# Second attention: the mirrored blocks of a chunk made by TensorE transposes, copied an item later

## The chip, the cores and the metric

The kernel runs on one core of one Trainium2 chip. The metric is the device time of one execution in microseconds, the median of several runs. Before the change it is 1772.9 us, the median of 3 runs (1772.55 to 1773.56).

## The reference

The input is 8 images of 128 channels and 48 x 48 positions (N = 2304 tokens). Layer 0 is a causal attention with projections; layer 1 is a second attention of the normalized tokens with themselves, and a recurrent layer behind it. The change concerns the second attention alone. Cut to what matters:

```python
def _L1_attn_ref(x):                       # x: (batch, tokens, 128), layer-normed
    attn = jnp.einsum('bnd,bmd->bnm', x / TEMPERATURE, x)
    attn = jax.nn.softmax(attn, axis=-1)
    out = jnp.einsum('bnm,bmd->bnd', attn, x)
    return out
...
x = x + _L0_conv_ref(_gn(x), ...)          # causal attention
t = _to_tokens(x)
t = t + _L1_attn_ref(_ln_t(t))             # second attention
t = t + _L1_ffn_ref(_ln_t(t), ...)         # batch norm and a recurrence over the tokens
```

The logits of the second attention are x times x transposed, so the matrix of logits is symmetric, and so are its exponentials before they are divided by the row sums.

## The kernel before, in words

All work is in fp32. The 2304 tokens of an image are 18 blocks of 128 (`NB`), or 6 chunks (`NQ`) of 384 columns (`QC`), each of 3 blocks (`QB`). Two classes make the two attentions: `Causal` (line 984) and `Full` (line 1118, the one that is changed). Each gives a list of items, one for each pair of a chunk j of queries and a block m of keys. In `Full`, an item is one of two kinds:

- *direct*: `begin` multiplies the block m by the chunk j (L1214, tile `s`, a PSUM bank of the pool `ps_s`), and ScalarE takes the exponential into a tile `p` of the pool `pp` (6 buffers), with a constant bias and with the sum over the columns into `rows[:, m, j]` (L1216). Then `product` multiplies `p` by the tokens of block m and adds it to the chunk's result `o` (L1228).
- *turned*: where the same pair of chunks was made before with the roles exchanged. VectorE has transposed the earlier `p` in pieces of 32 (L1177) and summed it (L1185), a DMA has stored it (`e`, L1157), another has loaded it (`g`, L1148); `begin` then makes no logits and `product` multiplies `g` (L1224).

Direct items of chunk j are those of the later chunks and of chunk j itself. The three of chunk j itself, the *own* items, are computed in full, 384 columns each, though of their nine blocks of 128 x 128 three are transposes of three others. I call the own items O0, O1, O2, other direct items D, and turned ones T. Chunk 0 begins O0 O1 O2 D D and so on. In later chunks the own items come last among the direct ones, and T are spread between by position:

```
1 D D D T D D D D D T D D D D O0 T O1 O2
2 D T D D T D D T D D T D D T O0 O1 T O2
3 D T D T D T D T D T D T O0 T O1 T O2 T
4 T D T T D T T D T T O0 T T O1 T T O2 T
5 T T O0 T T T T T O1 T T T T T O2 T T T
```

(The first figure is the chunk; O2 of chunk 5 stands among items of the next image's causal attention, which are put in between, at lines 1417 to 1421.)

The order of all work is written by hand (`manual_schedule`). One loop (lines 1426 to 1437) goes over the items of all images: at step n it calls `begin` of item n, then `product` of item n − 3 (`LAG = 3`), then `st.tick()`, which can issue up to two steps of the side chains. Each engine carries out its instructions in the order of issue:

```python
            if n < len(stream):
                part, j, what, first, last = stream[n]
                ready[n] = part.begin(j, what, first)
            if n >= LAG:
                part, j, what, first, last = stream[n - LAG]
                ...
                part.product(j, what, o[part, j], *ready.pop(n - LAG), first, last)
                ...
            st.tick()
```

`Stream` (line 548) is a planner: `spend` advances a planned TensorE clock, `then` plans when the other engines will be done, and a side chain's next step is issued once its planned time has come. Side chains carry the residuals, norms, projections (`pj`, L874 and L877) and the DMAs between them. A chunk's chain after its last product turns `o` back by TensorE transposes (`of_t`, L934), divides by the sums (`dn` from `rows`, L1254, and `ts`, L1259), and later multiplies by the first weight of the recurrent layer (`wx`, L1320); ScalarE has copies in it, `of` (L1246), `t2c` (L1341) and `wx` (L1326). The causal chains have `dn` (L1072) and `tb` (L934, read by L1105). Their PSUM tiles come from the pool `ps_t` (`psum_t`), which has two buffers used in turn.

Of the kernel before, what the change touches and what calls it, by code (L numbers as in the profile page):

```python
# [14 lines left out]
F32 = mybir.dt.float32  # L15
AF = mybir.ActivationFunctionType
ALU = mybir.AluOpType
AX = mybir.AxisListType
# [32 lines left out]
def general_path(ctx: ExitStack, tc: tile.TileContext, x, wq, bq, wk, bk, wv, bv, w_ffn, v_ffn, gamma, beta, pe, out):  # L51
# [44 lines left out]
    with ExitStack() as actx:  # L96
# [82 lines left out]
        def pop(n=1):  # L179
            for _ in range(n):  # L180
                if pend:
                    pend.popleft()()
# [195 lines left out]
        def full_attention(b, xhT, xh, done):  # L378
            xt = xbuf[b]
            LAG = 2  # L380

# [50 lines left out]
            for j in range(NQ):  # L432
                o = psum_o(f"o1_{b}_{j}")
                acc = work.tile([P, QC], F32, tag="acc", name=f"acc_{b}_{j}")
                ps = {}
                for m in range(NB + LAG):
                    if m < NB:
# [11 lines left out]
                    if j == 0 or m % 3 == 1:  # L449
                        pop()  # L450
                    if m >= LAG:
                        u = m - LAG
                        nc.tensor.matmul(o[:, :QC], xhT[:, u, :], ps.pop(u), start=(u == 0), stop=(u == NB - 1))
# [151 lines left out]
def fast_path(ctx: ExitStack, tc: tile.TileContext, x, pe, w_ffn, out, x_tok, w_qkv, w_pos, v_t, gamma_beta, flag):  # L605
    nc = tc.nc
    B, C, H, W = x.shape
    N = H * W
    P = 128
    assert C == P and N % P == 0  # L610
    NB = N // P
    CH = 512
    QC = 384
    NQ = N // QC
    QB = QC // P
    SCALE = 1.0 / math.sqrt(P)
    US = 4 / 2400.0
# [25 lines left out]
    ident = cpool.tile([P, P], F32, tag="ident", name="ident")  # L643
# [20 lines left out]
    with ExitStack() as actx:  # L664
# [11 lines left out]
        small2 = actx.enter_context(tc.tile_pool(name="small2", bufs=2))  # L676
# [4 lines left out]
        def psum_s(name):  # L681
            return ps_s.tile([P, CH], F32, tag="s", name=name)

        def psum_t(name):
            return ps_t.tile([P, CH], F32, tag="t", name=name)
# [13 lines left out]
        def psum_o(name):  # L699
            return ps_o.tile([P, CH], F32, tag="o", name=name)  # L700
# [28 lines left out]
        shift = apool.tile([P, 1], F32, tag="shift", name="shift")  # L729
# [46 lines left out]
        st = Stream()  # L776
# [207 lines left out]
        class Causal:  # L984
# [18 lines left out]
            def begin(self, j, m, first):  # L1003
                b = self.b
                if first:
                    st.finish(projected[b, j])
                    if j + EARLY < NQ:
                        project(b, j + EARLY)
                    if j == NQ - 1:
                        bounds(b)  # L1010
                off = self.offset(j, m)
                s = psum_s(f"s_{b}_{j}_{m}")
                nc.tensor.matmul(s[:, off:QC], keys[b][:, ts(m, P)], queries[b, j][:, off:], start=True, stop=True)  # L1013
                p = pp.tile([P, QC], F32, tag="p", name=f"p_{b}_{j}_{m}")
                nc.scalar.activation(p[:, off:], s[:, off:QC], AF.Exp, scale=SCALE)  # L1015
                ops = [("ACT", 0.16 + (QC - off) * 0.00085)]
                if m >= QB * j:
                    nc.gpsimd.tensor_mul(p[:, off : off + P], p[:, off : off + P], triu)  # L1018
                    ops.append(("POOL", 0.5))
                return p, st.then(st.spend((QC - off) * US), ops)  # L1020
# [97 lines left out]
        class Full:  # L1118
# [72 lines left out]
            def begin(self, j, what, first):  # L1191
                b = self.b
                if first and j == 0:
                    self.rows = small2.tile([P, NB, NQ], F32, tag="rows", name=f"rows_{b}")
                if j == 0:
                    st.finish(normed_chunks[b, what[1] // QB])
                if first and b + 1 < B:
                    if j == 1:
                        norm_chain[b + 1] = st.add(group_norm(b + 1))
                    if j == NQ - 2:  # L1200
                        st.finish(norm_chain[b + 1])
                        project(b + 1, 0)
                self.prefetch()
                if what[0] == "turned":
                    i, g = what[1:]
                    while (i, j) not in self.loaded:
                        while self.pairs[len(self.loaded)] not in self.stored:
                            self.store()
                        self.load()
                    return self.loaded[i, j][:, :, g, :, :].rearrange("p a m r -> p m a r"), 0.0  # L1210
                m = what[1]
                xh = x_hat[b][1]
                s = psum_s(f"s1_{b}_{j}_{m}")
                nc.tensor.matmul(s[:, :QC], xh[:, ts(m, P)], xh[:, ts(j, QC)], start=True, stop=True)  # L1214
                p = pp.tile([P, QC], F32, tag="p", name=f"p1_{b}_{j}_{m}")
                nc.scalar.activation(p, s[:, :QC], AF.Exp, bias=shift, accum_out=self.rows[:, m, j : j + 1])  # L1216
                return p, st.then(st.spend(QC * US), [("ACT", 0.58)])

            def product(self, j, what, o, p, ready, first, last):
                xhT = x_hat[self.b][0]  # L1220
# [13 lines left out]
            def after(self, j, o):  # L1234
                b, rows, tsum = self.b, self.rows, self.tsum
# [4 lines left out]
                if far:  # L1240
                    ot = turn_result(o, f"f_{b}_{j}", c, True)
                    at = st.then(st.now, [("DVE", 0.57)])
                    through = token_major(c, ot, f"f_{b}_{j}", "tof", 4)
                else:
                    o_sb = chunk_tile("o", f"of_{b}_{j}", c, 2)
                    nc.scalar.copy(o_sb, o[:, :QC])  # L1246
                    at = st.then(st.now, [("ACT", 0.5)])
# [3 lines left out]
                def sums():  # L1251

                    dn = small2.tile([P, QB], F32, tag="dn", name=f"dn_{b}_{j}")
                    nc.vector.tensor_reduce(dn, rows[:, QB * j : QB * (j + 1), : j + 1], AX.X, ALU.add)  # L1254
                    n = NQ - 1 - j
                    if n:
                        tp = psum_t(f"ts_{b}_{j}")
                        k = n * R * QB
                        nc.tensor.matmul(  # L1259
                            tp[:, :k], same.rearrange("p a c -> p (a c)"), tsum[j][:, :n, :].rearrange("p n k -> p (n k)"),  # L1260
                            start=True, stop=True,
                        )
                        own = small2.tile([P, NQ - 1, R, QB], F32, tag="own", name=f"own_{b}_{j}")
                        nc.vector.tensor_mul(
                            own[:, :n].rearrange("p n a g -> p (n a g)"), tp[:, :k], mine[:, :n].rearrange("p n a g -> p (n a g)")
                        )
                        more = small2.tile([P, QB], F32, tag="more", name=f"more_{b}_{j}")
                        nc.vector.tensor_reduce(more, own[:, :n].rearrange("p n a g -> p g (n a)"), AX.X, ALU.add)
                        nc.vector.tensor_add(dn, dn, more)
                    ri = small.tile([P, QB], F32, tag="ri", name=f"ri_{b}_{j}")  # L1270
                    nc.vector.reciprocal(ri, dn)
                    c["ri"] = ri
# [104 lines left out]
                else:  # L1377
# [7 lines left out]
                c["chain"] = self.before["chain"] = st.add([  # L1385
                    *through,
                    (sums, 0.15, [("DVE", 0.8)]),
                    (residual, 0.0 if far else 0.35, [("DVE", 3.2)]),
                    (rooted, 0.0, [("POOL", 0.9)]),
# [21 lines left out]


        LAG = 3
        stream = []
        for b in range(B):
            part, items = Causal(b), Causal.items()
# [5 lines left out]
            stream += [(part, *i) for i in items]  # L1422
            part = Full(b)
            stream += [(part, *i) for i in part.items()]
        ready, o = {}, {}
        for n in range(len(stream) + LAG):
            if n < len(stream):
                part, j, what, first, last = stream[n]
                ready[n] = part.begin(j, what, first)
            if n >= LAG:  # L1430
                part, j, what, first, last = stream[n - LAG]
                if first:
                    o[part, j] = psum_o(f"o_{n}")
                part.product(j, what, o[part, j], *ready.pop(n - LAG), first, last)
                if last:
                    part.after(j, o.pop((part, j)))
            st.tick()
# [10 lines left out]
    with ExitStack() as rctx:  # L1448
# [89 lines left out]
        for t in range(-WARM, LS):  # L1538
            s = t % TZ
# [28 lines left out]
        off = rc.tile([P, 1], F32, tag="off", name="off")  # L1568
# [11 lines left out]
@with_exitstack  # L1580
def conv_attn_hybrid_kernel(ctx: ExitStack, tc: tile.TileContext, args, laid):


    nc = tc.nc
    fpool = ctx.enter_context(tc.tile_pool(name="flag", bufs=1))
    flag = fpool.tile([1, 1], mybir.dt.int32, tag="flag", name="flag")
    x, w_ffn, pe, out = (args[i] for i in (0, 7, 11, 12))
    fast_path(tc, x, pe, w_ffn, out, *laid, flag)
    redo = nc.values_load(flag[0:1, 0:1], min_val=0, max_val=1, skip_runtime_bounds_check_because="the flag is the result of a comparison")
    with tc.If(redo > 0):  # L1590
        general_path(tc, *args)
# [41 lines left out]
```

## Time and profile before

| what | us |
|---|---|
| median of the runs | 1772.9 |
| the profiled execution, its own time | 1774.48 |
| its span, first to last instruction | 1772.5 |
| TensorE (PE) busy | 1742.7 |
| VectorE (DVE) busy | 1302.8 |
| ScalarE (ACT) busy | 764.8 |
| logits of direct items (L1214), 1008 matmul instructions | 410.4 |
| their products (L1228), 1008 | 404.1 |
| products of turned items (L1224), 720 | 281.3 |
| exponentials of direct items (L1216), 504 | 292.4 |
| reads of their accumulator, 504 | 97.2 |

An fp32 product is two matmul instructions, so the 504 direct items show as 1008. A matmul's recorded duration contains the time in which the next one already streams, so the spacing of starts says more on what it costs TensorE than its duration. PE is matmul, PEld the weight loads ahead of them. "Idle before" in a group's line is the time that the engine stood still just before its instructions, with what ended it. A transpose on TensorE is one matmul instruction whose weights are the block and whose moving operand is the identity.

### The profile page before, as it was taken

The page shows a single profiled execution, that of the slowest core. Times are in us where ns is not written, and L with a number is a line of the kernel's source. Part 1 is how long each engine was busy: PE and PEld are TensorE (multiplying, and loading weights), DVE is VectorE, ACT ScalarE, POOL GpSimd, SP SyncE. Part 2 cuts the span into 40 slices and gives each one's busy share as a digit, 9 for nine tenths or more (in the row PEclk, how much of TensorE's full clock was granted, in tenths as well). Part 3 has the DMA queues.
Part 4 walks back from the last instruction along what each step waited for, and adds up shares of the span by engine and source line. Part 5 has one row for each costly group of instructions (what it writes and reads, how often), then busy time and mean ns, then how long its engine had stood idle before and what let it go on. Part 6 is the DMA issues. An engine that isn't in the chain of part 4 may idle for free.

```text
span 1772.5 us, 22223 instructions
## 1 busy us (share of the span) xinstructions
PE 1742.7 (98%) x6231; PEld 1093.2 (62%) x6231; DVE 1302.8 (74%) x3363; ACT 764.8 (43%) x1842; POOL 195.2 (11%) x303
## 2 busy tenths in 40 slices
PE   8999999999999999999999999999999999999996
PEld 5666566665666566665666656665666656665565
DVE  4868668876887668786687767876687866877467
ACT  2344434443345434444344433454344543444455
POOL 1110011100110001100111001100011001110006
PEclk8999999999999999999999999999999999999998
DMA  4405672257533584156732575335941468116768
GB/s 140 138 23 187 182 204 94 87 184 188 145 103 128 159 226 141 34 176 182 200 99 80 188 192 152 106 111 161 237 129 50 160 183 214 45 65 198 194 211 216
DMA packets 206056, 262.00 MB, mean 148 GB/s; under 512 B 90113, under 2 KB 175010, under 8 KB 205412
## 3 DMA queue, kind: packets, MB, share of 16 engines
q1 hardware_dynamic: 204972, 257.47, 49.4%
q0 software_dynamic: 720, 2.62, 1.0%
q8 instruction: 52, 0.85, 0.2%
q14 instruction: 80, 0.66, 0.1%
q10 hardware_dynamic: 232, 0.40, 0.1%
HBM read 150.24 MB, written 110.17 MB: 147 GB/s over the span
## 4 chain that ended last, share of the span: by engine, by line
PE 96%; DMA 1%; DVE 1%; ACT 0%; issue 0%; SPq 0%; POOL 0%; ACTq 0%; POOLq 0%; DVEq 0%
PE o L1228 18%; PE s L1214 18%; PE s L1013 17%; PE o L1024 17%; PE o L1224 13%; PE pj L874 4%; PE pj L877 2%; PE z L1547 2%; PE wx L1320 2%; PE of_t L934 1%; PE tb L934 1%; PE pb L832 0%; DMA x<-in_x_dram 0%; PE dn L1072 0%; PE ts L1259 0%
## 5 line engine op out<-in xcount | busy, mean ns | idle before, releaser
L1216 ACT ACTIVATE p<-s,shift 128x384 f32<-128x384 f32 x504 | 292.4, 580 | 479.7 <-PE s L1214 464.2
L1015 ACT ACTIVATE p<-s 128x384 f32<-128x384 f32 (+2 forms) x504 | 231.8, 460 | 424.8 <-PE s L1013 377.5
L1214 PE MATMUL s<-xh 128*128 128x384 f32 x1008 | 410.4, 489 | 0.0
L1228 PE MATMUL o<-p,xhT 128*128 128x384 f32 x1008 | 404.1, 488 | 5.9 <-ACT p L1216 5.9
L1013 PE MATMUL s<-q,k 128*128 128x384 f32 (+2 forms) x1008 | 381.5, 460 | 0.2 <-DVE k L884 0.2
L1024 PE MATMUL o<-p,vT 128*128 128x384 f32 (+2 forms) x1008 | 377.4, 456 | 0.0
L1224 PE MATMUL o<-g,xhT 128*128 128x384 f32 x720 | 281.3, 488 | 1.1 <-DMA g<-e 1.1
L1228 PEld LDWEIGHTS o<-p,xhT 128*128 128x128 f32 x1008 | 188.9, 190 | 133.8 <-ACT p L1216 10.5
L1024 PEld LDWEIGHTS o<-p,vT 128*128 128x128 f32 x1008 | 188.8, 190 | 114.7 <-issue 0.6
L1214 PEld LDWEIGHTS s<-xh 128*128 128x128 f32 x1008 | 186.2, 190 | 115.3
L1013 PEld LDWEIGHTS s<-q,k 128*128 128x128 f32 x1008 | 182.6, 191 | 97.3 <-issue 1.0
L1039 DVE TENSOR_TENSOR acc<-acc,p 128x384 f32<-128x384 f32 (+2 forms) x408 | 208.8, 512 | 33.4 <-POOL p L1018 8.7
L1177 DVE STREAM_TRANSPOSE t<-p 128x384 f32<-128x384 f32 x360 | 187.3, 550 | 37.6 <-ACT p L1216 32.8
L1224 PEld LDWEIGHTS o<-g,xhT 128*128 128x128 f32 x720 | 133.2, 190 | 83.7 <-DMA g<-e 1.3
L1185 DVE TENSOR_REDUCE tsum<-t 128x12 f32<-128x1152 f32 x120 | 162.3, 1353 | 4.2
L879 DVE TENSOR_TENSOR z<-pj,pb 128x384 f32<-128x384 f32 x144 | 78.8, 547 | 108.8 <-PE pj L874 92.4
L1018 POOL TENSOR_TENSOR p<-p,triu 128x128 f32<-128x128 f32 x144 | 72.5, 505 | 606.2 <-ACT p L1015 475.2
L1294 POOL TENSOR_TENSOR roots<-ve_f,mhalf 128x3 f32<-128x3 f32 x48 | 40.7, 849 | 521.8 <-DVE ve_f L918 521.8
L1216 ACT ACTIVATION_READ_ACCUMULATOR p<-s,shift 128x1 f32 x504 | 97.2, 193 | 0.0
L874 PE MATMUL pj<-xn,wT 128*128 128x384 f32 x192 | 79.7, 500 | 1.4 <-DVE xn L867 1.4
L924 POOL TENSOR_TENSOR rs_c<-ve_c,mhalf 128x3 f32<-128x3 f32 x48 | 45.1, 939 | 216.2 <-DVE ve_c L918 213.6
L1321 DVE TENSOR_TENSOR scale<-wx,scale 128x384 f32<-128x384 f32 x46 | 25.4, 551 | 56.1 <-PE wx L1320 50.3
(264 smaller groups left out, 1485.6 us busy)
## 6 DMA issues: line engine op xcount, KB each, us to landing
e<-t SPq DMA_DIRECT2D x120, 576.0 KB
g<-e SPq DMA_DIRECT2D x480, 144.0 KB
pb<-posb_d SPq DMA_DIRECT2D x46, 576.0 KB
t1t<-in_x_tok_dram SPq DMA_DIRECT2D x48, 192.0 KB
t_d<-tt SPq DMA_DIRECT2D x184, 48.0 KB
t2x<-t_d SPq DMA_DIRECT2D x46, 192.0 KB
scale<-rs SPq DMA_DIRECT2D x46, 192.0 KB
x<-in_x_dram SPq DMA_DIRECT2D x14, 576.0 KB
```

The source lines that it names most:

```text
L874: nc.tensor.matmul(ps[:, :QC], wT[:, j, :], xn, start=True, stop=True)
L879: nc.vector.tensor_add(z, ps[:, :QC], c["pb"][:, j, :])
L1013: nc.tensor.matmul(s[:, off:QC], keys[b][:, ts(m, P)], queries[b, j][:, off:], start=True, stop=True)
L1015: nc.scalar.activation(p[:, off:], s[:, off:QC], AF.Exp, scale=SCALE)
L1024: nc.tensor.matmul(o[:, off:QC], vals[b][:, ts(m, P)], p[:, off:], start=first, stop=last)
L1039: nc.vector.tensor_add(a[:, off:], a[:, off:], p[:, off:])
L1177: nc.vector.transpose(t[:, :, :, g, :].rearrange("p b j r -> p j b r"), p.rearrange("p (j b r) -> p j b r", j=QB, b=R))
L1185: nc.vector.tensor_reduce(self.tsum[j][:, n - j - 1, :], t.rearrange("p b j m r -> p (b j) (m r)"), AX.X, ALU.add)
L1214: nc.tensor.matmul(s[:, :QC], xh[:, ts(m, P)], xh[:, ts(j, QC)], start=True, stop=True)
L1216: nc.scalar.activation(p, s[:, :QC], AF.Exp, bias=shift, accum_out=self.rows[:, m, j : j + 1])
L1224: nc.tensor.matmul(out_ap, xhT[:, QB * i + g, :], p, start=first, stop=last)
L1228: nc.tensor.matmul(o[:, :QC], xhT[:, what[1], :], p, start=first, stop=last)
```

## The change

In an own item n of the chunk (n = 0, 1, 2), only the columns from block n on are multiplied and exponentiated: 384 for O0, 256 for O1, 128 for O2. The missing blocks are made from the earlier own items: a function `mirror` takes a PSUM tile of `psum_t`, transposes into it one block (O1) or two (O2) on TensorE, and ScalarE copies them into the left part of `p`, with their sum over the columns into a new column 0 of `rows`. The other columns of `rows` move up by one; column 0 is set to zero by GpSimd once for each image, and the reduction of `rows` takes one column more. The loop keeps the mirrors in a list and issues that of item n at step n + 2, after `begin` of item n + 2 and ahead of `product` of item n − 1; the product of item n follows a step later, as before. 144 transposes and 96 copies are added, and the planner is given costs for them.

```diff
             def begin(self, j, what, first):
                 b = self.b
                 if first and j == 0:
-                    self.rows = small2.tile([P, NB, NQ], F32, tag="rows", name=f"rows_{b}")
+
+                    self.rows = small2.tile([P, NB, NQ + 1], F32, tag="rows", name=f"rows_{b}")
+                    nc.gpsimd.memset(self.rows[:, :, 0:1], 0.0)
...
                 s = psum_s(f"s1_{b}_{j}_{m}")
-                nc.tensor.matmul(s[:, :QC], xh[:, ts(m, P)], xh[:, ts(j, QC)], start=True, stop=True)
+                n = m - QB * j if m // QB == j else 0
+                off = n * P
+                nc.tensor.matmul(s[:, off:QC], xh[:, ts(m, P)], xh[:, QC * j + off : QC * (j + 1)], start=True, stop=True)
                 p = pp.tile([P, QC], F32, tag="p", name=f"p1_{b}_{j}_{m}")
-                nc.scalar.activation(p, s[:, :QC], AF.Exp, bias=shift, accum_out=self.rows[:, m, j : j + 1])
-                return p, st.then(st.spend(QC * US), [("ACT", 0.58)])
+                nc.scalar.activation(p[:, off:], s[:, off:QC], AF.Exp, bias=shift, accum_out=self.rows[:, m, j + 1 : j + 2])
+                ready = st.then(st.spend((QC - off) * US), [("ACT", 0.36 + (QC - off) * 0.0006)])
+                if m // QB != j:
+                    return p, ready
+                if n == 0:
+                    self.own = []
+                own = list(self.own)
+                self.own.append((p, ready))
+
+                def mirror():
+
+                    tp = psum_t(f"mi_{b}_{j}_{n}")
+                    for i, (q, at) in enumerate(own):
+                        nc.tensor.transpose(tp[:, ts(i, P)], q[:, ts(n, P)], ident)
+                        end = st.spend(P * US / 2, at)
+                    nc.scalar.activation(p[:, :off], tp[:, :off], AF.Copy, accum_out=self.rows[:, m, 0:1])
+                    return st.then(end, [("ACT", 0.36 + off * 0.0006)])
+
+                return (p, ready, mirror) if n else (p, ready)
...
-                    nc.vector.tensor_reduce(dn, rows[:, QB * j : QB * (j + 1), : j + 1], AX.X, ALU.add)
+                    nc.vector.tensor_reduce(dn, rows[:, QB * j : QB * (j + 1), : j + 2], AX.X, ALU.add)
...
         LAG = 3
+        MIRROR = 1
...
-        ready, o = {}, {}
+        ready, o, late = {}, {}, deque()
...
-                ready[n] = part.begin(j, what, first)
+                *ready[n], more = (*part.begin(j, what, first), None)[:3]
+                if more:
+                    late.append((n, more))
+            while late and late[0][0] < n - MIRROR:
+                i, more = late.popleft()
+                ready[i][1] = more()
```

## The prediction

> **What bounds the kernel now.** I read the page's busy times first, then its chain that ended last.
>
> ```profile
> PE 1742.7 (98%) x6231; PEld 1093.2 (62%) x6231; DVE 1302.8 (74%) x3363; ACT 764.8 (43%) x1842; POOL 195.2 (11%) x303
> PE 96%; DMA 1%; DVE 1%; ACT 0%; issue 0%; SPq 0%; POOL 0%; ACTq 0%; POOLq 0%; DVEq 0%
> ```
>
> TensorE is the bound from end to end: 96% of the chain is PE. So every column that PE doesn't stream is time won, and every wait put on PE is time lost. PE busy time is modelled, so I price PE by the pitch between starts, in a stretch of the timeline where all shapes stand side by side (PE, then the ACT row of it):
>
> ```profile
> 83.56 0.49 PE L934 MATMUL tb<-ident,xhT 128*128 128x128 f32 x3
> 83.89 0.60 PE L1013 MATMUL s<-q,k 128*128 128x256 f32 x2
> 84.32 0.81 PE L1024 MATMUL o<-p,vT 128*128 128x384 f32 x2
> 84.97 0.38 PE L1013 MATMUL s<-q,k 128*128 128x128 f32 x2
> 85.19 0.49 PE L1024 MATMUL o<-p,vT 128*128 128x384 f32 x1
> ...
> 84.09 0.48 ACT L1105 COPY xh<-tb 128x384 f32<-128x384 f32 x1 [0.48 <-PE tb L934]
> ```
>
> A product of 384 columns holds PE 0.65 us (84.97 less 84.32; in long rows 0.645), one of 256 columns 0.43, one of 128 columns 0.22, and three transposes together 0.33, thus 0.11 each. Weight loads add nothing to a short product here. ACT starts 0.20 us after PE has moved on (84.09 less 83.89).
>
> Next the groups by shape (engine, operation, count, busy us, mean ns, idle before), for what ACT pays:
>
> ```profile
> L1216 ACT ACTIVATE p<-s,shift 128x384 f32<-128x384 f32 x504 | 292.4, 580 | 479.7 <-PE s L1214 464.2 <-PE o L1228 8.8 <-DVE st_c L915 5.6
> L1216 ACT ACTIVATION_READ_ACCUMULATOR p<-s,shift 128x1 f32 x504 | 97.2, 193 | 0.0
> L1015 ACT ACTIVATE p<-s 128x384 f32<-128x384 f32 x408 | 200.1, 490 | 358.9 <-PE s L1013 330.8 <-DVE acc L1035 15.2 <-DVE acc L1039 7.7
> L1015 ACT ACTIVATE p<-s 128x256 f32<-128x256 f32 x48 | 18.4, 383 | 42.9 <-PE s L1013 27.5 <-DVE acc L1039 15.2
> L1015 ACT ACTIVATE p<-s 128x128 f32<-128x128 f32 x48 | 13.3, 277 | 23.1 <-PE s L1013 19.2 <-DVE acc L1039 2.0 <-DVE mv_c L916 1.0
> ```
>
> The bias of L1216 costs 0.09 us over L1015 at 384 columns. Last, what a late `p` does to PE (a stretch of the timeline, other engines left out):
>
> ```profile
> 1029.22 0.81 PE L1224 MATMUL o<-g,xhT 128*128 128x384 f32 x2
> ...
> 1030.42 0.19 ACT L1216 ACTIVATION_READ_ACCUMULATOR p<-s,shift 128x1 f32 x1
> ...
> 1030.66 0.30 PEld L1228 LDWEIGHTS o<-p,xhT 128*128 128x128 f32 x2 [1.25 <-ACT p L1216]
> ...
> 1031.41 0.81 PE L1214 MATMUL s<-xh 128*128 128x384 f32 x2
> ```
>
> The weight load waits for the accumulator's read (end 1030.61), not for the ACTIVATE. The next product starts at 1031.41, so this one had its slot from 1030.765 instead of 1029.87: 0.9 us lost. So from the read's end to PE's slot it is 0.15 us, and from an ACTIVATE's start to its read's end 0.67 (0.10 before the ACTIVATE's end, plus 0.19). The waits list has 8 such, 5.9 us in all.
>
> **What the Trainium skill says.** "TensorE: Matmul & The Clock Gate", Terms, calls transpose mode 4 times faster for fp32; the trace gives 0.11 against 0.215 us, twice, and I use that. Its Part 4 says that a transpose lands in PSUM and needs a copy, about 275 ns: the records say 273, but three in a row take 0.33. "ScalarE: Activation LUTs", What ACT_TABLE_LOAD costs, has 186 ns + 0.833 N and 93 ns for a pointer bias: 293 for 128 columns, the trace 277, and 90 for the bias. Its Table sets section puts copy into every set; the trace agrees in that copies and exponentials alternate and only two table loads (1.28 us each) occur in the whole run.
>
> **The change, part by part.** In each of 48 chunks (8 images, 6 chunks) the own blocks are items O0, O1, O2. O, D (other direct) and T (turned) name items of the stream; "mirror" is the transposes and their copy.
>
> *Logits.* O1 streams 256 columns, O2 128: saved 0.215 + 0.43 = 0.645 us of PE a chunk, 48 times: −31.0.
>
> *Transposes.* One for O1, two for O2: 3 x 0.11 = 0.33 a chunk, 48 times: +15.8. Their inputs were made two or more items before, so they don't wait for them. Gross −15.1 (−31.0 + 15.8, rounded terms).
>
> *ACT.* Shorter exponentials save 0.09 + 0.21 us; the copies with an accumulator take about 0.37 (128 columns: 0.277 − 0.10 + 0.19) and 0.47 (256). No row shows a copy with an accumulator; L1015's shapes, which have no bias either, are the nearest, and I take them; with a pointer bias' 0.09 more it would be 0.46 and 0.56, and below L1015 nothing speaks for it. ACT is 43% busy: its sum costs nothing, its lateness does.
>
> *The new wait.* The copy follows the exponential of item n+2 on ACT, and PE's product of n waits for it in order, with all later PE work behind it. On ACT the next exponential is queued behind the copy, which itself waits at most about 0.4 us for the transposes, while that exponential's logits need 0.64 more on PE: free. From the transposes' slot end, an idle ACT needs 0.20 + 0.37 + 0.15 = 0.72 us (O1) or 0.82 (O2). Behind a full exponential (starts 0.20 after its logits' slot, frees ACT 0.65 later), it is 0.85 + 0.37 + 0.15 = 1.37 from those logits, for O2 1.47; behind O2's short one (0.44 for 0.65) 1.16.
> What PE has in between comes from the item order: the product of n−1, the logits of n+3 if n+3 is direct, the mirror of n+1 if that is O2. I laid the order of every chunk over the trace, image by image:
> chunk 0 (O0 O1 O2 D D D): 1.29 or more after the transposes, needs 1.26 and 1.25: no wait.
> chunk 1: O1 has D, then T at n+3: logits end, 0.11 + 0.645 + 0.22 = 0.975 later PE wants it, ready at 1.37: 0.395 lost.
> chunk 2: none (1.29 on both).
> chunk 3: O1 has O2, then T: 0.11 + 0.645 = 0.755 against 1.16: 0.405. O2 has 1.29: none.
> chunk 4: none, as long as a projection of the next image (L877) stands in O2's window (0.65 of cover; without it 0.17).
> chunk 5: O2 is followed by the next image's causal block: 0.43 (256 columns) against 0.82: 0.39. O1 has a projection in its window (without it 0.07).
> That is 1.19 an image. The last image differs: chunk 1 as above (0.4), chunk 3 no wait, chunk 4 0.42 (L1341 stands on ACT), chunk 5 some 0.55, because its mirror needs a PSUM buffer that L1341 frees late. In sum 7 x 1.19 + 1.4 = +9.7.
>
> *PSUM.* Mirrors take the two buffers of psum_t in turn with dn, ts, of_t, tb and wx. Before each mirror's place the older of the two had been read at least 0.3 us before, in all but that one case: 0, up to 2 us for each collision if chains move.
>
> *Zeroing, one more column.* The POOL memset has no row; POOL products take 0.5 to 1.0 us, and it may queue behind one such. O0's product is 3 us later: 0, at most 1 us in 8 places. The dn reduction (122 ns, 48 times) grows by 3 elements: nothing.
>
> *Moved steps.* The planner's clock advances less per own item, so chain steps (sums, residual, fetch, stores of t and loads of g, on SP too) can come one item earlier or later, past copies and exponentials on ACT and DMA issues on SP. PE waited for `g` once, 1.1 us, so SP has cover; a slip is 0 to ±1 us an image.
>
> Sum: −15.1 + 9.7 = −5.4. The profiled execution took 1774.5 us (span 1772.5, the rest lies around it and stays), giving 1769.1; it is 1.6 above the median of 1772.9, so 1767.5 on the median's scale.
>
> **Rivals.** *In time everywhere*: other chains' PE work comes to cover the three tight places, as L877 does in chunk 4, and the present 5.9 us of waits move off: −15.1, or 1757.8; with half of the 9.7 left, 1762.7. Against: none of the three has a chain's PE step in its window in any of the first seven images.
> *One more collision an image*: L1341 and L1326 (ACT copies of 1.13 us, 46 times each) already lie in the windows of chunks 3 and 4. One slid ahead of a mirror's copy costs 1.13 less 0.1 to 0.6 of slack, about 0.75; 8 of them give −5.4 + 6.0 = +0.6: 1773.5, no change.
> *Slower*: the same mechanism twice or more an image, since mirrors have 0.7 to 1.3 us of slack where exponentials have three items: at 16 places +12.0 − 5.4 = +6.6, 1779.5. It outweighs the gain from 8 places on and shows as slower from 12. For it: L1326 waits for DVE up to 2.6 us (19.0 in all) with ACT held. Against: in the present order ACT is free at every mirror but for the exponential.
> *It doesn't do what it says*: a table load for each copy, 96 x 1.28 us = 123 and more. The two loads of the whole run speak against it.
>
> **How the numbers follow.** A measurement of this kernel tells about 0.2%, 3.5 us. As read (1764.5 to 1769.3): 0.46, faster. In time: 0.12, faster. One collision (1769.4 to 1776.4): 0.26, same. Slower: 0.14, plus 0.02 for table loads. Faster 0.58, same 0.26, slower 0.16. The range, 1760 to 1776.4, leaves out slower and the table loads (0.16) and the deepest of in time (0.04).
>
> **What would show it.** L1214's group should split into 384, 256 and 128 columns, with 144 transposes at 0.11 pitch. PE's wait for ACT at L1228 should rise from 5.9 us by about 9, in the chunks named. Were it 15 or more, with L1341 or L1326 before it, the slower rival holds; PE waiting on psum_t's readers would be a cost that I put at nothing.

## The result and the profile after

| | time, us | ratio to before, 95% interval |
|---|---|---|
| before, measured beside it | 1773.23 | |
| after | 1773.27 | 1.0005 [0.9988, 1.0022] |
| forecast | 1767.5 | 0.997 |

No difference that this measurement can tell, and the forecast's ratio lies outside the interval. The profiled execution took 1773.78 us with a span of 1772.1 (before: 1774.48 and 1772.5). The 15 us of TensorE work that the change takes out are gone from PE, and about the same amount of waiting stands on PE in their place. In the page of the changed kernel, busy times and the chain that ended last:

```profile
PE 1734.7 (98%) x6375; PEld 1096.0 (62%) x6375; DVE 1308.8 (74%) x3363; ACT 786.2 (44%) x2034; POOL 213.1 (12%) x311
PE 92%; DMA 3%; SPq 2%; ACT 1%; DVE 1%; issue 0%; POOL 0%; ACTq 0%; POOLq 0%; DVEq 0%
```

PE's share of the chain fell from 96% to 92%; what came in is mostly DMA and SP's queue. Second, the groups by shape (engine, operation, count, busy us, mean ns, idle before) of the changed kernel:

```profile
L1218 PE MATMUL s<-xh 128*128 128x128 f32 x96 | 18.4, 274 | 0.0
L1233 PE MATMUL mi<-ident,p 128*128 128x128 f32 x144 | 31.4, 273 | 0.0
L1235 ACT ACTIVATE p<-mi 128x256 f32<-128x256 f32 x48 | 18.4, 383 | 22.1 <-PE mi L1233 21.6
L1235 ACT ACTIVATION_READ_ACCUMULATOR p<-mi 128x1 f32 x96 | 18.9, 197 | 0.0
L1347 ACT COPY wx<-scale 128x384 f32<-128x384 f32 x46 | 52.0, 1131 | 1.7 <-DVE scale L1342 0.8
```

The split and the 144 transposes are as forecast, and the mirror's copy costs what L1015's rows cost (0.27 and 0.38 us, plus the accumulator's read). The last line wasn't forecast: in the kernel before, the copy of `scale` into `wx` (L1326 there) held ACT 19.0 us in waiting for DVE; now 0.8. Third, the waits on PE (us in total, times, longest):

```profile
PE o L1245 <- DMA g<-e: 5.2, 9, 1.0
PE s L1218 <- ACT xh L1105: 4.5, 8, 0.6
PE o L1249 <- ACT p L1235: 2.1, 1, 2.1
```

Before, the first line of this list was 5.9 us of `p`: seven waits in chunk 3, which have gone, and one of 1.5 us in the last image, which stayed (the third line, 2.1). Of the mirrors only one wait, in the last image, is in this list; the others stand on the weight load, in a list of its own (10.9 us, 24 times). The two largest waits, for `g` and for `xh`, belong to steps that the diff doesn't name.

Therefore I count PE by pitch, as the prediction did: start of an instruction less start of the one before it, less the pitch of its shape; a wait adds 0.10 us more in the second of the two matmuls. Per image, in us (g(i,5) is the load of turned blocks that chunk 5 takes from chunk i; "first seven" are images 0 to 6, since no next image stands behind the last):

| what PE waits for | before | after | forecast |
|---|---|---|---|
| chunk 3, first D: `p`, ACT held by the `wx` copy | 0.90 (7 images) | 0 | as before |
| chunk 1, O1: mirror's copy | – | 0.31 (8) | 0.395 |
| chunk 3, O1: mirror's copy | – | 0 | 0.405 |
| chunk 5, O2: mirror's copy | – | 0.40 (7) | 0.39 |
| chunk 0, logits of block 15: `xh` | 0 | 0.83 (8) | 0 |
| chunk 5, turned items: g(3,5) | 0 | 0.3 to 1.1 in five, mean of seven 0.4 | 0 |
| chunk 5, turned items: g(0,5) | 0 | 1.1 and 1.3 in images 2 and 5, 0.2 in two others, mean 0.4 | 0 |

An image loses 1.89 us of work (the gross gain, 15.1 / 8). So the first seven should move by 7 x (−1.89 − 0.90 + 0.31 + 0.40 + 0.83) + 5.8 (all their waits for `g`) = −3.0 us; from the first product of the second attention in image 0 to that in image 7 the changed kernel gains 2.6 us. (It also comes there 1.1 us earlier in image 0: −3.7 in all.) In the last image and the tail it gives this back: −2.2 at the last product, −0.4 at the end of the span.

The wait for `xh` is the clearest case of a moved step. The timeline of the kernel before, then of the changed kernel, at the same place (PE's transposes `tb`, ACT's copy `xh`, PE's next logits):

```profile
554.70 0.49 PE L934 MATMUL tb<-ident,xhT 128*128 128x128 f32 x3
555.02 0.81 PE L1214 MATMUL s<-xh 128*128 128x384 f32 x2
555.67 0.81 PE L1228 MATMUL o<-p,xhT 128*128 128x384 f32 x2
556.32 0.81 PE L1214 MATMUL s<-xh 128*128 128x384 f32 x2
```

```profile
553.98 0.49 PE L934 MATMUL tb<-ident,xhT 128*128 128x128 f32 x3
554.51 0.48 ACT L1105 COPY xh<-tb 128x384 f32<-128x384 f32 x1 [0.30 <-PE tb L934]
555.04 0.91 PE L1218 MATMUL s<-xh 128*128 128x384 f32 x2 [0.57 <-ACT xh L1105]
```

The logits of block 15 are the first that read these columns of `xh`: the fourth line of before, with a pair of logits and a product between; in the changed kernel they are next after `tb`, and PE waits for the copy. The planner's clock advances less in the own items, so the step comes an item later, right ahead of the logits that need it.

The wait for g(3,5) is another moved step, on SP's queue (start, duration, issues), again before and after, in image 6, chunk 5, with PE's wait in the last line:

```profile
1466.22 7.17 SPq L1148 DMA_DIRECT2D g<-e  x8
1473.98 1.55 SPq L1305 DMA_DIRECT2D rs<-roots_t  x3
1475.75 1.84 SPq L1308 DMA_DIRECT2D t_d<-tt  x4
1477.69 3.70 SPq L1148 DMA_DIRECT2D g<-e  x8
```

```profile
1462.11 11.10 SPq L1148 DMA_DIRECT2D g<-e  x12
1473.31 1.56 SPq L1326 DMA_DIRECT2D rs<-roots_t  x3
1474.91 1.87 SPq L1329 DMA_DIRECT2D t_d<-tt  x4
1476.88 2.90 SPq L1148 DMA_DIRECT2D g<-e  x4
...
1482.46 0.88 PE L1245 MATMUL o<-g,xhT 128*128 128x384 f32 x2 [0.85 <-DMA g<-e]
```

Four issues are one load of `g`. Before, `spread` (the `rs` and `t_d` issues of chunk 3, 3.4 us of the queue) stood ahead of g(2,5) and g(3,5), and these two went out one right behind the other; now it stands between them. So g(3,5) has `spread` ahead of it in both kernels; what is new is that g(2,5) goes first and g(3,5) has to follow `spread`. Counted from PE's first product with g(0,5), the last issue of g(3,5) comes after 5.7 to 7.4 us, before after 4.4 to 5.4. PE also wants it sooner, since 1.3 us of the next image's projections (`pj`) no longer stand in between: it came there after 10.9 us before, now after 9.6 to 10.5, its wait included. PE took g(3,5) 5.5 to 6.5 us after its last issue before, and now 3.1 to 3.9 after it, having waited in five of the seven images.

None of this explains the wait for g(0,5), the other half of what PE waits for `g`. It stands ahead of `spread` in both kernels, and in images 2 and 5 PE waited for it until 8.5 and 9.0 us after its last issue. No experiment isolates its cause.

### The profile page after: what moved, and what is told of

It is laid out like the page before. It is cut to its first block, busy times and chain, and to the rows that moved or that the text cites. A ratio compares the mean times of both kernels' runs of the same rounds, so it can differ in the third digit from the quotient of the medians.

```text
span 1772.1 us, 22688 instructions
## 1 busy us (share of the span) xinstructions
PE 1734.7 (98%) x6375; PEld 1096.0 (62%) x6375; DVE 1308.8 (74%) x3363; ACT 786.2 (44%) x2034; POOL 213.1 (12%) x311
## 4 chain that ended last, share of the span: by engine, by line
PE 92%; DMA 3%; SPq 2%; ACT 1%; DVE 1%; issue 0%; POOL 0%; ACTq 0%; POOLq 0%; DVEq 0%
PE o L1249 18%; PE s L1013 17%; PE o L1024 17%; PE s L1218 16%; PE o L1245 11%; PE pj L874 3%; DMA g<-e 2%; PE z L1574 2%; PE pj L877 2%; PE wx L1341 2%; SPq L1148 1%; PE tb L934 1%; PE of_t L934 1%; PE mi L1233 1%; PE pb L832 0%
## 5 line engine op out<-in xcount | busy, mean ns | idle before, releaser
L1220 ACT ACTIVATE p<-s,shift 128x384 f32<-128x384 f32 (+2 forms) x504 | 277.6, 551 | 448.0 <-PE s L1218 446.0
L1015 ACT ACTIVATE p<-s 128x384 f32<-128x384 f32 (+2 forms) x504 | 230.7, 461 | 411.1 <-PE s L1013 364.3
L1218 PE MATMUL s<-xh 128*128 128x384 f32 (+2 forms) x1008 | 381.2, 460 | 4.5 <-ACT xh L1105 4.5
L1245 PE MATMUL o<-g,xhT 128*128 128x384 f32 x720 | 285.6, 489 | 5.2 <-DMA g<-e 5.2
L1249 PEld LDWEIGHTS o<-p,xhT 128*128 128x128 f32 x1008 | 185.7, 190 | 119.6 <-ACT p L1235 10.9
L1245 PEld LDWEIGHTS o<-g,xhT 128*128 128x128 f32 x720 | 129.1, 190 | 79.4 <-issue 13.0
L1018 POOL TENSOR_TENSOR p<-p,triu 128x128 f32<-128x128 f32 x144 | 85.0, 592 | 589.6 <-ACT p L1015 584.9
L1315 POOL TENSOR_TENSOR roots<-ve_f,mhalf 128x3 f32<-128x3 f32 x48 | 45.2, 942 | 519.3 <-DVE ve_f L918 519.3
L1302 DVE SCALAR_TENSOR_TENSOR t<-of_t,ri,t1t 128x128 f32<-128x128 f32 x144 | 41.6, 344 | 47.1 <-PE of_t L934 47.1
```

What stands on the lines that cost most here:

```text
L1218: nc.tensor.matmul(s[:, off:QC], xh[:, ts(m, P)], xh[:, QC * j + off : QC * (j + 1)], start=True, stop=True)
L1220: nc.scalar.activation(p[:, off:], s[:, off:QC], AF.Exp, bias=shift, accum_out=self.rows[:, m, j + 1 : j + 2])
L1245: nc.tensor.matmul(out_ap, xhT[:, QB * i + g, :], p, start=first, stop=last)
L1249: nc.tensor.matmul(o[:, :QC], xhT[:, what[1], :], p, start=first, stop=last)
```

## The experiments

My theory after the result: the arithmetic pays what was forecast, the mirror waits cost somewhat less, and the rest is lost through the planner, whose costs the change also edits and which moves other steps. The rival: steps moved or not, PE that is ahead runs into transfers whose speed is fixed (in chunks 4 and 5 of image 2 the DMA engines are 0.8 to 0.95 busy), so any gain would be given back.

### 1. The planner charged as before

```diff
-                ready = st.then(st.spend((QC - off) * US), [("ACT", 0.36 + (QC - off) * 0.0006)])
+                ready = st.then(st.spend(QC * US), [("ACT", 0.58)])
...
-                        end = st.spend(P * US / 2, at)
...
-                    return st.then(end, [("ACT", 0.36 + off * 0.0006)])
+                    return ready
```

> The changed kernel, but its planner is charged as in the kernel before (full columns for every own item, nothing for a mirror), so that every side chain, DMA and projection stands at the same item as before. Theory A, that what ate the gain is the moved steps (the logits wait for xh, 0.83 us an image, and the loads of g): both waits are gone, the old wait of 0.9 us an image behind the wx copy is back, mirror waits are 0.3 to 0.4 us in chunks 1, 3 and 5, and the time is 15.1 less 9.7 = 5 us below before, 1768. Rival R, that PE merely ran ahead into loads that the DMA engines can't bring sooner: the waits for g stay at 5 us or more whatever the order, 1773.

Measured 1776.57 us, 1.0016 [1.0009, 1.0023], above both expectations. The waits for `xh` and `g` were gone from the first seven images, as the theory has it, and the old wait of chunk 3 was back (0.9), but chunk 1 lost 1.24 us in every image instead of 0.4. The trace, ACT and then PE:

```profile
168.90 0.58 ACT L1220 ACTIVATE p<-s,shift 128x384 f32<-128x384 f32 x1 [1.76 <-PE mi L1233]
169.47 0.27 ACT L1234 ACTIVATE p<-mi 128x128 f32<-128x128 f32 x1
```

```profile
168.53 0.38 PE L1233 MATMUL mi<-ident,p 128*128 128x128 f32 x2
169.88 0.59 PE L1248 MATMUL o<-p,xhT 128*128 128x384 f32 x1 [0.97 <-ACT p L1234]
```

An exponential waits for a transpose, not for its logits. It writes into one of the six buffers of `p`, here the one that held O0's, and the last reader of that is now O2's mirror. ACT stands still 1.76 us, the mirror's copy of O1 queues behind, and PE waits. A resource that I hadn't listed at all: the mirrors keep O0's and O1's `p` in use for longer.

### 2. The moved steps alone

```diff
-                nc.tensor.matmul(s[:, off:QC], xh[:, ts(m, P)], xh[:, QC * j + off : QC * (j + 1)], start=True, stop=True)
+                nc.tensor.matmul(s[:, :QC], xh[:, ts(m, P)], xh[:, ts(j, QC)], start=True, stop=True)
...
-                        nc.tensor.transpose(tp[:, ts(i, P)], q[:, ts(n, P)], ident)
...
-                    nc.scalar.activation(p[:, :off], tp[:, :off], AF.Copy, accum_out=self.rows[:, m, 0:1])
```

(and the exponential over 384 columns; the zeroing and the extra column of `rows` stay in.)

> The arithmetic of the kernel before (full logits, no transposes, no copies), with the planner charged as in the changed kernel, so that only the placement of side chains and DMAs changes. Theory A: the xh wait of 0.83 us appears in 8 images (+6.7), the old wait of 0.9 us goes (-7), and the loads of g, placed later on SP, are late by up to 0.8 us an image: 1773 to 1779. Rival R: no wait for g, since PE isn't ahead; 1773.

Measured 1782.52 us, 1.0042 [1.0026, 1.0058]: with the arithmetic of before, the planner's new costs alone take 7.5 us, of which about 4 arise in the first seven images (0.6 an image) and the rest in the last image and the tail. PE's waits (us in total, times, longest):

```profile
PE s L1218 <- ACT xh L1105: 4.5, 8, 0.6
PE o L1242 <- DMA g<-e: 4.2, 6, 1.0
```

PE waits for `xh` 0.83 us in all 8 images and for g(3,5) 0.4 to 1.3 in six of the first seven, and the old 0.9 is gone, as in the changed kernel. PE isn't ahead here, so being ahead isn't what makes g(3,5) late: its last issue comes 6.3 to 7.4 us after PE's first product with g(0,5). For g(0,5) there is no wait here, so that one can't be put down to the planner's costs alone.

### 3. Planner as before, mirrors one item earlier

```diff
-        MIRROR = 1
+        MIRROR = 0
```

(on top of 1.)

> As e1, and each mirror is issued one item earlier (MIRROR = 0), so that its copy has one more product as cover. Theory A: the mirror waits go too, and nearly all of the 15.1 us is left: 1758 to 1760. Rival R: g waits of 5 us or more: 1763 to 1765.

Measured 1763.25 us, 0.994 [0.9927, 0.9954]: faster than both kernels. A chunk without a wait is 0.31 us shorter than before, an image 1.40 (1.89 less 0.38 that chunk 1 still waits, in seven images). The rest of an image's 1.89 is 0.1 to 0.4 us of `g` in three of the first seven images. The time lies in the range that the rival had given, but not for its reason: PE is ahead by 1.4 us an image, and what is still lost is mostly the 0.38 of chunk 1 and the old 0.9 of chunk 3.

### 4. The transposes and copies as an addition

Logits and exponentials in full; the mirrors are made too, into other columns of the same PSUM tile, and not used; the planner is charged as in 1, and the reduction leaves out the new column. The copy:

```diff
-                    nc.scalar.activation(p[:, :off], tp[:, :off], AF.Copy, accum_out=self.rows[:, m, 0:1])
+                    nc.scalar.activation(tp[:, 2 * P : 2 * P + off], tp[:, :off], AF.Copy, accum_out=self.rows[:, m, 0:1])
```

> The kernel before with full logits, plus the 144 transposes and 96 copies with accumulators at the places of the changed kernel, into PSUM that no product reads, planner as before: the price of the added work without a wait for it. By the pitch of 0.11 us: +15.8 us, 1789. A rival, that transposes between products cost more than three in a row (a weight load that isn't covered, 0.1 us more each): +30 us, 1803.

Measured 1791.71 us, 1.0091 [1.0075, 1.0106]. In the trace each image grows by 1.99 us, 0.33 a chunk and 0.11 a transpose, and no new wait appears: the price of the transposes was right, and 96 copies cost ACT nothing that PE sees as long as no product waits for them.

### 5. `xh` an item earlier

```diff
-                    st.finish(normed_chunks[b, what[1] // QB])
+                    st.finish(normed_chunks[b, min(what[1] + 1, NB - 1) // QB])
```

> The changed kernel, but chunk 0 asks for the normalised input's transpose (tb and its ACT copy xh) one item before the first logits that read it; its order of steps is otherwise left to the planner. Theory (moved steps): in the changed kernel tb stands right in front of the logits of block 15, which wait 0.73 + 0.10 us for the ACT copy in each of the 8 images; in the kernel before one item stands between. With the item back, 8 x 0.83 = 6.7 us go: about 1766.6 us, and the PE wait for ACT xh (4.5 us, 8 times) is gone from the list; the waits for g (about 0.7 us an image) remain. Rival: the normalisation on VectorE isn't ready an item earlier, so PE waits for it instead: about 1773 us.

Measured 1766.46 us, 0.9954 [0.994, 0.9968]. The wait for `xh` is gone from the trace, and nothing took its place; the waits for g(3,5) stayed (0.2 to 0.7 us in six images, 2.1 and more in image 6). Those for g(0,5) are gone here, although PE is further ahead; why, the run doesn't show, and its gain isn't that of `xh` alone. Asking earlier also moves the planner's clock a little, so other steps shift as well, but no other wait came or went in the first four chunks. One step put back by one item gives more than the gain that was forecast for the whole change.

### 6. Seven buffers for `p`

```diff
-        pp = actx.enter_context(tc.tile_pool(name="pp", bufs=6))
+        pp = actx.enter_context(tc.tile_pool(name="pp", bufs=7))
...
-        small2 = actx.enter_context(tc.tile_pool(name="small2", bufs=2))
+        small2 = actx.enter_context(tc.tile_pool(name="small2", bufs=1))
```

(on top of 1; the second edit makes the room.)

> The first experiment (changed kernel, planner charged as before, 1776.6 us) with seven buffers for p instead of six; room for it comes from one buffer instead of two for the small tiles rows, tsum, own, dn and more. Theory (buffers of p): in chunk 1 the exponential of the first block after the own ones takes over the buffer of the first own block's p, whose last reader is now the mirror of the third block, so it starts 1.6 us late and the mirror's copy behind it too: PE waits 1.24 us. With a seventh buffer the wait falls to 0.3 to 0.4 us, as in the changed kernel: 8 x 0.85 to 0.93 = 6.8 to 7.4 us less, about 1769.5 us. Rival: ACT is late there for another reason (the copy's own queue): the wait stays and the time is about 1776.5; single buffers for the small tiles could add waits on DVE and ACT, up to 1 us an image.

Measured 1768.76 us, 0.9965 [0.9951, 0.9979], against 1.0016 in experiment 1. Chunk 1 waits 0.31 us, and no exponential waits for a mirror any more: the buffer was the cause. Chunk 3's O1 waits 0.38 here, forecast 0.405: with the order of before that term was right. PE waits 0.5 to 0.6 us for `g` in three of the first seven images, twice for g(0,5) and once for g(2,5): with the planner as before such waits arise without moved steps.

### 7. Stores of `t2c` on another queue

```diff
-                        nc.sync.dma_start(t2s_d[:, g - 1, b], self.t2c)
+                        nc.scalar.dma_start(t2s_d[:, g - 1, b], self.t2c)
```

(and the two stores of `out` and `t2l_d` likewise, on top of the changed kernel.)

> The changed kernel with the stores of t2c (three or four transfers an image) issued from ScalarE's queue, right behind the copies that write t2c, in place of SyncE's; nothing else differs. Theory (queue): on SP these stores now stand ahead of loads of g and wait there for t2c (59.5 us in all, 11.3 before), which makes the loads late; off SP, PE's waits for g in chunk 5 (0.2 to 1.2 us an image in the first seven) go: about 4.5 us less, 1768.8 us, while the xh wait of 0.83 us an image stays. Rival 1: the loads are late by their own place or by the DMA engines' load (0.9 busy there), and the waits stay: 1773. Rival 2: the issues hold ACT (0.4 to 2 us each) and make exponentials late: 1775 to 1780.

Measured 1787.2 us, 1.0062 [1.0047, 1.0076]: a miss. PE's waits for `g` grew to 13.1 us. In SP's list of waits stands a line that the changed kernel doesn't have:

```profile
SPq L1157 <- DMA out_dram<-t2c: 36.2, 7, 6.9
```

A store of `e`, with the loads of `g` behind it, now waits for the end of the store that I had moved away. Why an `e` store depends on it the trace doesn't say. So the run tells nothing on whether the stores' old place made `g` late; I dropped that reading for the order of `spread`. (In experiment 12 the stores stand on SP's queue and hold it for 56.4 us, and g(3,5) is in time.)

### 8. The `wx` copy of chunk 0 on GpSimd

```diff
-                    nc.scalar.copy(wx[:, :, b, ts(j, SJ)], c["scale"].rearrange("p (s l) -> p l s", l=LS))
+                    copy = nc.scalar.copy if j else nc.gpsimd.tensor_copy
+                    copy(wx[:, :, b, ts(j, SJ)], c["scale"].rearrange("p (s l) -> p l s", l=LS))
```

(on top of 3.)

> The third experiment (MIRROR = 0, planner charged as before, 1763.25 us), with chunk 0's copy of scale into wx made by GpSimd instead of ScalarE (8 of 46 such copies). Theory: the wait of 0.9 us in chunk 3 (7 images) is ACT held by that copy while it waits for VectorE's scale; off ACT, it goes: 6.3 us less, about 1757 us. Rival: GpSimd's copy takes several us or disturbs VectorE, or other exponentials wait instead: 1762 to 1766 us.

Measured 1762.66 us, 0.9933 [0.9919, 0.9946]; the theory had 1757. The wait of chunk 3 is gone in all seven images, but five of them now wait 0.4 to 1.1 us for g(0,5). Here the rival has its part: with 2.4 us an image to be won and 1.6 kept, the loads' slack in this order is used up.

### 9. `xh` earlier and `spread` forced back

```diff
+                if (i, j) == (2, 5):
+                    st.advance(self.chain[3], 5)
```

(in `load`, on top of 5; two further lines keep each chunk's chain in `self.chain`.)

> The fifth experiment (xh an item earlier, 1766.46 us) with one more moved step put back: chunk 3's spread (seven DMA issues of rs and t2_d, 3.2 us of SP's queue) stands again ahead of the load of g for blocks 2 of chunk 5, instead of between that load and the one for blocks 3. Theory (queue): in the changed kernel PE wants g(3,5) 3.1 to 3.9 us after the load's last issue, against 5.5 to 6.8 before, and waits 0.2 to 2.1 us for it in chunk 5 of the first seven images (5 us in the fifth experiment); with the step back these waits go: 4 to 5 us less, about 1762 us. Rival (throughput): the transfer engines are the limit in chunks 4 and 5, so the same waits come back at another load: 1765 to 1767 us.

Measured 1784.39 us, 1.0052 [1.0039, 1.0065]: a miss, and the wrong way. g(3,5) was in time, but g(2,5) now came 2.4 to 3.1 us late in each of the seven images. SP's waits, then PE's:

```profile
SPq L1329 <- DVE roots_t L1323: 50.3, 14, 6.1
```

```profile
PE o L1248 <- DMA g<-e: 19.3, 8, 3.0
```

The place was that of the kernel before, but in this order of the other steps `roots_t` isn't ready there; SP waits for it (18.4 us in experiment 5) with two loads behind. So an issue that waits on SP's queue makes the loads behind it late; whether the place of before cures g(3,5), this run can't tell, since PE comes to it late anyway.

### 10 and 11. The ninth with MIRROR = 0, and the eighth with seven buffers

On top of 9, and on top of 8:

```diff
-        MIRROR = 1
+        MIRROR = 0
```

```diff
-        pp = actx.enter_context(tc.tile_pool(name="pp", bufs=6))
+        pp = actx.enter_context(tc.tile_pool(name="pp", bufs=7))
...
-        small2 = actx.enter_context(tc.tile_pool(name="small2", bufs=2))
+        small2 = actx.enter_context(tc.tile_pool(name="small2", bufs=1))
```

> The ninth experiment with MIRROR = 0: the transposes follow the block's own logits by one item less. Theory (mirror waits): the waits of PE for the mirror's copy, 0.31 us in chunk 1 and 0.40 in chunk 5 of an image, go: 5.3 us less than the ninth, about 1756.5 us. Rival (queue): the planner's order moves once more, and the load of posb (576 KB) now stands ahead of the load of g(3,5); that load is late by the 1 to 3 us which it takes, in each of seven images: 1763 to 1775 us.

> The eighth experiment (1762.66 us) with seven buffers for p (and one for the small tiles). Theory (buffers of p): the wait of 0.27 + 0.10 us in chunk 1 of seven images comes from the third own block's exponential taking the first own block's p; with a seventh buffer it goes: 2.6 us less, about 1760 us. Rival (throughput of chunk 5's loads): what is won in chunk 1 is waited for at g, where the eighth already waits 0.4 to 1.1 us an image: no change, 1762 to 1763 us.

Measured 1779.73 us, 1.0023 [1.0014, 1.0031], and 1771.47 us, 0.9981 [0.9974, 0.9987]; both outside what theory and rival had given. In 10 the mirrors wait no more in the first seven images, but PE waits for `g` in each image, up to 2.1 us at once, and for a causal `p` 0.65 in six. In 11 the wait in chunk 1 is gone, and waits of 1.6 us in all stand in chunk 2: with MIRROR = 0 the seventh buffer changes which buffer is taken where, and more exponentials than before wait for a mirror. ACT's list:

```profile
ACT p L1220 <- PE mi L1233: 31.3, 15, 3.5
```

(16.2 us at 9 places in experiment 1, 15.0 at 9 in experiment 8, none in 6.)

### 12. `xh` earlier and `spread` later

```diff
-                        (turn_root, 0.0, [("DVE", 0.15)]),
-                        (spread, 0.0, [("", 10.0)]),
+                        (turn_root, 0.0, [("DVE", 0.15), ("", 3.5 if j == 3 and b < B - 1 else 0.0)]),
+                        (spread, 0.0, [("", 10.0 - (3.5 if j == 3 and b < B - 1 else 0.0))]),
```

(on top of 5.)

> The fifth experiment (1766.46 us) with chunk 3's spread (seven DMA issues, 3.4 us of SP's queue) planned 3.5 us later in the first seven images, so that it stands behind the load of g for blocks 3 of chunk 5; in the ninth, where it was forced ahead of the load for blocks 2, SP waited there for VectorE's roots_t and PE then for g(2,5), 2.4 to 3.1 us an image. ACT's order doesn't differ from the fifth. Theory (queue): g(3,5) is issued 3.4 us earlier, and the waits for it in chunk 5 (0.2 to 0.7 us in six images, 2.5 in one) go: about 4.5 us less, 1762 us. Rival (throughput or buffers): the load of g(3,5) has to wait for its buffer, or that of g(4,5) or of posb gets late instead: 1765 to 1769 us.

Measured 1762.43 us, 0.9922 [0.9909, 0.9936]: the lowest time, though the intervals of experiments 3 and 8 overlap with it. SP's queue in image 2, then what is left of `g` in PE's waits, then the chain that ended last:

```profile
632.95 14.57 SPq L1148 DMA_DIRECT2D g<-e  x16
647.62 1.74 SPq L1326 DMA_DIRECT2D rs<-roots_t  x3
649.41 1.86 SPq L1329 DMA_DIRECT2D t_d<-tt  x4
```

```profile
PE o L1245 <- DMA g<-e: 0.2, 1, 0.2
```

```profile
PE 96%; DMA 1%; DVE 1%; ACT 1%; issue 0%; SPq 0%; POOL 0%; ACTq 0%; POOLq 0%; DVEq 0%
```

Four loads stand ahead of `spread`, PE takes g(3,5) 5.2 us after its last issue, and the chain has 96% PE again. PE still wants g(3,5) as early, but its last issue is back at 4.3 us after PE's first product with g(0,5), and that suffices. The 0.2 us left are for g(0,5), in one image. An image now gains 1.95 us against before; by the table it should be 1.89 + 0.90 − 0.31 − 0.40 = 2.08.

## Why the prediction was right or wrong

The time lay inside the range, at its upper end, but in the case that the prediction gave 0.26; the case that it held likeliest, −0.3%, didn't come. By the prediction's own steps:

- *Logits and transposes*, −31.0 and +15.8: right. Experiment 4 measured 0.33 us a chunk for the transposes, experiment 3 a chunk shorter by 0.31.
- *ACT*: right; the copies are as priced, and their sum cost nothing.
- *The new wait*, 1.19 an image: mis-sized, 0.71 in the changed kernel. Chunks 1 and 5 have 0.31 and 0.40 for 0.395 and 0.39. Chunk 3's 0.405 doesn't occur, because moved steps changed what stands there; with the order of before it is 0.38 (experiment 6). In that order the waits can also be far longer than forecast, by a buffer of `p` (1.24 in experiment 1): a step that the prediction lacked.
- *PSUM, zeroing, one more column*: nothing of them shows in PE's waits.
- *Moved steps*, "a slip is 0 to ±1 us an image", counted as nothing: this is the step that failed. In experiment 2, where they stand alone, its parts are +0.83 (`xh`), about +0.65 (g(3,5)) and −0.90 (the `wx` copy no longer holds ACT), 0.6 an image, plus the last image's and the tail's: 7.5 us, more than the forecast's whole gain. In the changed kernel g(3,5) takes 0.4 an image, and g(0,5) another 0.4, which experiment 2 doesn't have. "PE waited for `g` once, 1.1 us, so SP has cover" took a missing wait for slack without measuring it: where PE waited, g(3,5) took 3.1 to 3.8 us from its last issue to its product; it had had 5.5 to 6.5, and an issue some 2 us later and a use 1.3 us sooner use that up.
- *The rivals*: "one more collision" gave 1773.5, nearly the measured time, but its mechanism, a copy of 1.13 us ahead of a mirror's copy, is nowhere in the first seven images; the number agrees by chance. The part of "in time" that said that the present 5.9 us move off came true for chunk 3, and helped hide the loss (its −15.1 doesn't count them).

The cause of the loss in the first seven images is shown by taking it away: experiment 5 for `xh`, experiment 12 for g(3,5), and experiment 2 that both come from the planner's costs and not from the arithmetic. Left open are two things. The waits for g(0,5), 2.8 us in these images, come and go with runs that didn't aim at them: experiments 3, 6 and 8, with the planner as before, have some, experiments 2 and 5 have none, and 12 has one of 0.3. There the rival, PE running ahead into transfers, is neither shown nor ruled out; experiment 12, with the largest gain an image, speaks against it. The other is the 3.3 us that the changed kernel gives back in the last image and the tail. Its waits there are for `xh` (0.83), g(2,4) (0.35, none before), g(1,5) and g(2,5) (1.1 and 0.65, before 1.2 and 0.24) and O2's product (2.3, 1.7 before). Experiment 2, with the arithmetic of before, loses 4.3 there, experiment 5 2.7, and experiments 3 and 6, with the planner as before, nothing; so most of it goes with the order, but the tail wasn't taken apart. (Experiment 1 loses 2.2, with 1.1 of a wait for `p` in chunk 2.)

## What to carry to other kernels

When a change alters the costs that a planner works with, the order of every later step is part of the change: list the instructions whose place moves, engine by engine and queue by queue, and for each the slack of who waits for it, measured from its issue to its use. An edit that reads a tile again later also lengthens the life of its buffer, and the next writer waits in silence on another engine. And test the arithmetic and the order apart: here one takes 15 us of work off TensorE, and the other alone costs 7.5.

## What was not expected of the hardware

- From its last issue to its product the same load of 4 x 144 KB took very different times: g(3,5) 3.1 to 3.8 us where PE waited for it, g(0,5) 8.5 and 9.0. So one load's slack says nothing on another's. The three `rs` issues of 0.5 KB hold SP's queue 1.6 to 1.8 us, as long as the four of a `g` load where nothing delays them (1.8).
- Every ACTIVATE with an accumulator is followed by a read of 193 to 197 ns, copies too, and the weight load of a waiting product starts after the read, not after the ACTIVATE.
